# Seven edits to a four-layer transformer kernel: later FP4 weights, spreads of sixteen rows, carries copied by ScalarE, one masked product, stored positions

## The chip, the cores and the metric

The kernel runs on one core of a Trainium2 chip. The metric is the device time of one execution in microseconds (us), the median of three timed runs. The engines are named as in the profile: PE is TensorE (PEld its weight loads), DVE is VectorE, ACT is ScalarE, POOL is GpSimd, and SP is SyncE, which here only issues DMAs.

## The reference

Eight sequences of 1024 rows by 256 columns, all float32, pass through four blocks, each added to its input after a layernorm:

1. a decoder layer with causal linear attention of 16 heads of 16 columns, whose flows are normalised by running sums, followed by a GELU MLP 256 to 1024 to 256;
2. a ReLU MLP 256 to 1024 to 256;
3. softmax attention with one head of 256 columns over the 1024 rows;
4. a gated MLP 256 to 704 to 256, whose inputs and weights are rounded block by block to FP4 and back.

The part that the change touches most is the linear attention of block 1:

```python
sink_in  = normal / einsum(q + EPS, cumsum(k) + EPS)
src_out  = normal / einsum(k + EPS, cumsum(q) + EPS)
cons_sink = einsum(q + EPS, cumsum(k * src_out) + EPS) / normal
cons_src  = einsum(k + EPS, cumsum(q * sink_in) + EPS) / normal
src_comp = exp(clip(cons_src)) / cumsum(exp(clip(cons_src))) * normal
kv = cumsum(k (x) (v * src_comp));  x = (q * sink_in / normal) kv * sigmoid(cons_sink)
```

`normal` is the position in the sequence, 1 to 1024. The einsums sum over the 16 columns of a head.

## The kernel before

**Tiling.** A chunk is 128 rows, a group is G = 4 chunks (GT = 512 rows), and a sequence is NG = 2 groups, so there are 16 groups, p = 0 to 15. Group p runs through `linear_group(p)` (linear attention), `dense` (both MLPs of blocks 1 and 2, 64 steps of 256 rows by 128 hidden columns per group, each with its own pair of weight loads `w_ff`, five buffers deep), `norms_1` and `norms_2`. Then `soft_chunk` does blocks 3 and 4 chunk by chunk once a sequence has passed its two groups.

**Order of the work.** All of it is written out at build time by a planner, `Plan`. Parts are generators that yield what they need next (an engine, tiles, a free buffer, a due time `at`). `Plan.run` picks the part that waits least by a model of the engines, then the ripest, then by `at`, issues its instructions, and `Plan.took` (L157) books their modelled cost. Every engine's queue is then pinned to that order. So a step that is removed, added or priced differently can change the order of everything behind it, on every engine, SP's DMA queue included.

**Linear attention of a group.** `linear_span` (L919) projects q and k for all rows of its span, transposed: head and column on the partitions, row on the free axis. Tiles `cur[0..1]` are q, `cur[2..3]` are k. Then, in order:

- For each of the four tiles, a running sum (`running`, L806: one scan on DVE, and a copy of its last column into a carry for the next span if there is one) and a product with the tile of the other kind. `head_sums` adds 16 partitions of each head on PE.
- `flow` is position over these sums (L983). It has one row per head, and is needed on all 16 partitions of a head. In the first group, which is split in two spans (`near`), PE spreads it with masks. In the other 15 groups `spread` (L763) writes it to DRAM (`packed`) and reads it back four times with a repeating pattern (tiles `spread`, 128 x 512).
- Scale k and q by it, again four running sums and products, and `head_sums`.
- Clip, exp, a running sum on DVE, a reciprocal, and `scale` (L1040 to L1046), which is spread in the same manner to two tiles that scale q.

A carry is copied only where another span of the sequence follows: in both spans of group 0 and in every other even group, 8 times a span, 72 in all.

`linear_chunk` (L1079) then does the masked scores, the output, and the running k times v: the 32-column product `kvbank` is multiplied by a block-diagonal mask `bdiag` into `kv`, in two instructions (L1219), 112 in all.

**FP4 weights.** `fp4_weights` (L645) loads 18 pieces of the FP4 weights (`w_raw`), rounds them on DVE and ACT, and transposes them on PE. Piece i has `at = 0.9 + 2.2 i / 18`. In units of `at`, group p's linear work lies at p + 0.1 to p + 0.75, its dense work at p + 1 to p + 2, and the softmax of the first sequence from 3.

**Positions.** `pos` holds 1 to 512 as float; `rpos` is the reciprocal of position for both groups of a sequence (L501), made in `late_constants`.

Of the kernel before, what the change touches and what calls it, by code (L numbers as in the profile page):

```python
# [62 lines left out]
class Plan:  # L63
# [12 lines left out]
    def __init__(self, tc, nc):  # L76
# [15 lines left out]
        self.tiled = False  # L92
        self.parts = []
# [63 lines left out]
    def took(self, queue, op, args, kw):  # L157
# [44 lines left out]
        for ap in aps:  # L202
            name = ap.tensor.name
            if self.by.get(name) != queue:
                start = max(start, self.done.get(name, 0.0))
            if name not in self.done and name in self.held:
                start = max(start, self.used[name])
        end = start + cost
        if queue == "sync":
            n = 4e-6 / 160e-3  # L210
# [116 lines left out]
def block_stack_kernel(ctx: ExitStack, tc: tile.TileContext, a: dict, out: bass.AP):  # L327
# [115 lines left out]
    pos = const.tile([P, P], F32, name="pos")  # L443
    nc.vector.tensor_copy(pos, pos_i)
# [38 lines left out]
    def late_constants():  # L483
# [15 lines left out]
        for g in range(NG):  # L499
            yield dve()  # L500
            nc.vector.tensor_scalar(rpos[:, g, :], pos, float(g * GT), None, ALU.add)  # L501
            yield dve()
            nc.vector.reciprocal(rpos[:, g, :], rpos[:, g, :])
# [141 lines left out]
    def fp4_weights():  # L645
# [15 lines left out]
        for i, (src, turns) in enumerate(pieces):  # L661
            for j in range(i, min(i + 3, len(pieces))):
                if j not in raws:
# [3 lines left out]
                        dma(at=0.9 + 2.2 * i / len(pieces), when=lambda: count["stage"] == 4),  # L667
# [7 lines left out]
            at = 0.9 + 2.2 * i / len(pieces)  # L675
# [87 lines left out]
    def spread(packed, tiles):  # L763


        width = packed.shape[0] // 32 * P
        flat = hbm.tile([32, GT], F32, tag="packed", name="packed", bufs=4)
        yield dma(packed)
        nc.sync.dma_start(
            out=flat[:, :width].rearrange("r (t l) -> t r l", l=P), in_=packed  # L770
        )
        out = {}
        for b in tiles:
            t = out[b] = yield from fresh("flow", dma(flat), "spread")
            nc.sync.dma_start(
                out=t[:, :width],
                in_=bass.AP(
                    tensor=flat.tensor,
                    offset=flat.offset + 8 * b * GT,
                    ap=[[GT, 8], [0, DH], [1, width]],  # L780
# [25 lines left out]
    def running(out, cur, carry, b, first, last):  # L806
# [9 lines left out]
        if not last:  # L816
            nc.vector.tensor_copy(carry[:, b : b + 1], out[:, cur.shape[1] - 1 :])
# [101 lines left out]
    def linear_span(p, span, fronts, tiles):  # L919
# [48 lines left out]
        for n, b in enumerate((2, 0, 3, 1)):  # L968
            other = (b + 2) % 4
            prods[other] = yield from fresh(  # L970
                "flow", dve(cur[b], at=p + 0.15 + 0.04 * n + after, when=turn("flow")), "prod"
            )
            prod = prods[other][:, :width]
            running(prod, cur[b], past["cur"], b, opens, closes)
            yield dve(cur[other])
            nc.vector.scalar_tensor_tensor(prod, cur[other], ATT_EPS, prod, ALU.add, ALU.mult)
# [6 lines left out]
        nc.vector.scalar_tensor_tensor(flow, pos[rows], float(g * GT), r1, ALU.add, ALU.mult)  # L983
# [638 lines left out]
```

## Time and profile before

| what | value |
| --- | --- |
| time, median of three runs | 2690.91 us (2689.86 to 2692.45) |
| the profiled execution | 2683.94 us, of which the span from first to last instruction is 2682.2 us |
| mean granted PE clock | 0.991 |
| busy: PE, PEld, DVE | 2597.4, 2014.0, 1969.3 us |
| busy: ACT, POOL | 1246.7, 560.5 us |
| DMA | 209.92 MB, mean 78 GB/s |
| dense steps of group 0, first to last matmul of the first layer | 72.3 to 175.6 us |
| the same of groups 1, 2, 3 | 184.1 to 277.5; 286.2 to 432.1; 434.0 to 589.1 us |
| last dense step of group 15 | 2505.8 us |
| first softmax chunk starts; last one ends | 300.0; 2678.7 us |

Busy time is a sum over the whole span. The first group has the core to itself, the dense work starts at 72.3 us, the softmax chunks join at 300 us, and after 2505.8 us only softmax chunks are left. The time of the profiled execution is 1.74 us above its span and 6.97 us under the median of the runs.

In the rows of the profile, "idle before" or a figure in square brackets is the time for which the engine sat idle just before the instruction, and behind "<-" stands what ended it. Since every instruction goes through one helper, all lines read L308, and the tiles' names tell them apart.

### The profile page before, as it was taken

Reading aid. Unit: us, or ns where it says so; the run is one execution under the profiler, and the core shown is the slowest. Engines: PE = TensorE matmul, PEld = TensorE weight load, DVE = VectorE, ACT = ScalarE, POOL = GpSimd, SP = SyncE. Lnnn points to the kernel's source line nnn. Section 1 sums busy time; section 2 is a strip of 40 time slices with the busy share of each in tenths; the row PEclk is TensorE's granted clock in tenths of the full one; section 3 lists DMA queues with packets and bytes.
Section 4 is the critical chain, followed back from the end, with each engine's and each line's share of the span. In section 5 each row is a group of like instructions: output and inputs, shape, how many; then the busy total and the mean of one; then the engine's idle time right before and its main releaser. Section 6 shows DMA issues by size and latency. Waiting matters only on the chain.

```text
span 2682.2 us, 45602 instructions
## 1 busy us (share of the span) xinstructions
PE 2597.4 (97%) x16687; PEld 2014.0 (75%) x16687; DVE 1969.3 (73%) x4514; ACT 1246.7 (46%) x2430; POOL 560.5 (21%) x1101
## 2 busy tenths in 40 slices
PE   6999999999999999999999999999999999999997
PEld 4777777777777777777777777777777777787765
DVE  8889687776858668686776858778586776856576
ACT  2443445535455453645536354363635536344343
POOL 1232232221212213122131212212121131212000
PEclk8999999999999999999999999999999999999999
DMA  3334222312223222232322223132231322322100
GB/s 87 107 105 143 89 82 64 108 59 89 73 69 106 66 86 73 69 96 71 91 73 76 80 75 106 52 92 75 70 108 54 98 63 71 89 66 81 41 12 12
DMA packets 282135, 209.92 MB, mean 78 GB/s; under 512 B 23864, under 2 KB 270392, under 8 KB 281912
## 3 DMA queue, kind: packets, MB, share of 16 engines
q1 hardware_dynamic: 281912, 207.00, 25.9%
q8 instruction: 133, 2.18, 0.3%
q14 instruction: 90, 0.74, 0.1%
HBM read 188.17 MB, written 18.74 MB: 77 GB/s over the span
## 4 chain that ended last, share of the span: by engine, by line
PE 80%; DVE 12%; DMA 2%; issue 1%; ACT 1%; POOL 1%; SPq 0%; DVEq 0%; ACTq 0%
PE bank L308 80%; DVE hid L308 2%; DVE prod L308 1%; DVE n L308 1%; DVE ln_st L308 1%; DMA spread<-packed 1%; DVE x_amax L308 1%; DVE u L308 1%; DMA w_ff<-in_L_attn_W_dram 1%; DVE res L308 1%; POOL ln_rstd L308 1%; DVE div L308 1%; DVE e L308 0%; DVE q L308 0%; DVE ln_mv L308 0%
## 5 line engine op out<-in xcount | busy, mean ns | idle before, releaser
L308 PE MATMUL bank<-half,w_ff 128*128 128x256 f32 x2048 | 533.6, 383 | 14.5 <-DMA w_ff<-in_L_ffn_w_dram 6.0
L308 PE MATMUL bank<-w_ff,hidden 128*128 128x256 f32 x2048 | 530.4, 383 | 7.7 <-issue 6.6
L308 PEld LDWEIGHTS bank<-half,w_ff 128*128 128x128 f32 x2048 | 379.4, 191 | 91.4 <-issue 26.6
L308 PEld LDWEIGHTS bank<-w_ff,hidden 128*128 128x128 f32 x2048 | 371.1, 191 | 96.0 <-issue 50.7
L308 ACT ACT_TABLE_LOAD x308 | 395.2, 1283 | 75.2 <-PE bank L308 71.1
L308 POOL TENSOR_SCALAR ln_ve<-ln_mv 128x1 f32<-128x1 f32 x384 | 96.0, 250 | 1320.7 <-DVE ln_mv L308 1299.4
L308 ACT ACTIVATE hidden<-bank,c_L_ffn_b 128x256 f32<-128x256 f32 x256 | 121.1, 473 | 338.0 <-PE bank L308 336.7
L308 PE MATMUL bank<-n2T,qT 128*128 128x512 f32 x512 | 241.4, 594 | 0.9 <-ACT qT L308 0.9
L308 POOL TENSOR_TENSOR ln_rstd<-ln_ve,neghalf 128x1 f32<-128x1 f32 x384 | 229.4, 597 | 32.0
L308 PE MATMUL bank<-vt,probT 128*128 128x256 f32 x1024 | 232.2, 380 | 0.0
L308 PEld LDWEIGHTS bank<-vt,probT 128*128 128x128 f32 x1024 | 193.2, 190 | 30.3 <-issue 3.3
L308 ACT ACTIVATE hidden<-bank,c_L_attn_b 128x256 f32<-128x256 f32 x256 | 121.4, 474 | 177.0 <-PE bank L308 175.4
L308 PE MATMUL bank<-wdT,hqT 128*128 128x256 f32 x768 | 178.0, 382 | 1.8 <-ACT hqT L308 1.8
L308 PE MATMUL bank<-wgT,xqT 128*128 128x352 f32 x512 | 173.4, 461 | 1.1 <-ACT xqT L308 0.9
L308 PE MATMUL bank<-wuT,xqT 128*128 128x352 f32 x512 | 172.4, 459 | 0.0
L308 DVE TENSOR_TENSOR sc<-bank,triu 128x512 f32<-128x512 f32 x256 | 159.4, 679 | 5.3 <-PE bank L308 3.8
L308 PEld LDWEIGHTS bank<-wdT,hqT 128*128 128x128 f32 x768 | 145.4, 191 | 22.8 <-ACT hqT L308 2.8
L308 DVE TENSOR_TENSOR hid<-hid,bank 128x352 f32<-128x352 f32 x118 | 60.9, 516 | 133.8 <-PE bank L308 92.0
L308 POOL TENSOR_TENSOR xr<-xr,b_L_attn_ln_b 128x256 f32<-128x256 f32 x64 | 49.3, 788 | 482.6 <-DMA xr<-in_L_attn_inputs_dram 482.6
L308 PEld LDWEIGHTS bank<-n2T,qT 128*128 128x128 f32 x512 | 93.6, 190 | 69.5 <-issue 62.7
L308 PEld LDWEIGHTS bank<-wuT,xqT 128*128 128x128 f32 x512 | 97.3, 190 | 54.2
L308 PEld LDWEIGHTS bank<-wgT,xqT 128*128 128x128 f32 x512 | 92.6, 190 | 37.0 <-issue 3.8
(214 smaller groups left out, 4384.4 us busy)
## 6 DMA issues: line engine op xcount, KB each, us to landing
w_ff<-in_L_attn_W_dram SPq DMA_DIRECT2D x512, 128.0 KB
w_ff<-in_L_ffn_w_dram SPq DMA_DIRECT2D x512, 128.0 KB
spread<-packed SPq DMA_DIRECT2D x90, 256.0 KB
x<-in_L_attn_inputs_dram SPq DMA_DIRECT2D x64, 128.0 KB
xr<-in_L_attn_inputs_dram SPq DMA_DIRECT2D x64, 128.0 KB
rows<-res SPq DMA_DIRECT2D x64, 128.0 KB
out_dram<-y SPq DMA_DIRECT2D x64, 128.0 KB
rows<-rows SPq DMA_DIRECT2D x56, 128.0 KB
```

Of the source, the lines that this page charges most:

```text
L308: ins = method(*args, **kw)
```

## The change

Seven edits:

1. `spread` writes `packed` twice, side by side, into a DRAM tile of [32, 2, 512], and the four (or two) reads take a pattern of 16 rows, each repeated 8 times, where they took 8 rows, each repeated 16 times. Source and destination bytes of a spread stay 256 KB.
2. `running` leaves the copy of the carry to ACT, as a planned step of its own. In `linear_span` the four tiles go in two pairs: two scans, then the two products.
3. `pos` holds the positions of both groups; `rpos` and `flow` read it without an addition.
4. The two instructions that multiply e by position and by the row mask `src` become one.
5. The two masked products of k times v become one instruction of 256 elements.
6. The pieces of the FP4 weights have `at = 1.5 + 1.6 i / 18`.
7. The planner's model: a DMA moves 250 bytes per ns instead of 160, and PE costs twice as much for 2.1 us after more than 2 us of modelled idleness.

```diff
@@ Plan.took
+        if queue == "tensor":
+            if start - self.ran > 2.0:
+                self.slow = start + 2.1
+            if start < self.slow:
+                cost *= 2
+            self.ran = start + cost
         end = start + cost
         if queue == "sync":
-            n = 4e-6 / 160e-3
+            n = 4e-6 / 250e-3
@@ constants, late_constants
-    pos = const.tile([P, P], F32, name="pos")
-    nc.vector.tensor_copy(pos, pos_i)
+    pos = const.tile([P, NG, P], F32, name="pos")
+    for g in range(NG):
+        nc.vector.tensor_scalar(pos[:, g, :], pos_i, float(g * GT), None, ALU.add)
...
-            nc.vector.tensor_scalar(rpos[:, g, :], pos, float(g * GT), None, ALU.add)
-            yield dve()
-            nc.vector.reciprocal(rpos[:, g, :], rpos[:, g, :])
+            nc.vector.reciprocal(rpos[:, g, :], pos[:, g, :])
@@ fp4_weights (twice)
-            at = 0.9 + 2.2 * i / len(pieces)
+            at = 1.5 + 1.6 * i / len(pieces)
@@ spread
-        width = packed.shape[0] // 32 * P
-        flat = hbm.tile([32, GT], F32, tag="packed", name="packed", bufs=4)
+        flat = hbm.tile([32, 2, GT], F32, tag="packed", name="packed", bufs=4)
         yield dma(packed)
-        nc.sync.dma_start(
-            out=flat[:, :width].rearrange("r (t l) -> t r l", l=P), in_=packed
-        )
+        for e in range(2):
+            nc.sync.dma_start(out=flat[:, e, :].rearrange("r (t l) -> t r l", l=P), in_=packed)
...
-                    offset=flat.offset + 8 * b * GT,
-                    ap=[[GT, 8], [0, DH], [1, width]],
+                    offset=flat.offset + 8 * b * 2 * GT,
+                    ap=[[GT, 16], [0, DH // 2], [1, GT]],
@@ running
         if not last:
-            nc.vector.tensor_copy(carry[:, b : b + 1], out[:, cur.shape[1] - 1 :])
+            yield act(out)
+            nc.scalar.copy(carry[:, b : b + 1], out[:, cur.shape[1] - 1 :])
@@ linear_span, running sums of the tiles (those of the weighted tiles likewise)
-        for n, b in enumerate((2, 0, 3, 1)):
-            other = (b + 2) % 4
-            prods[other] = yield from fresh(
-                "flow", dve(cur[b], at=p + 0.15 + 0.04 * n + after, when=turn("flow")), "prod"
-            )
-            prod = prods[other][:, :width]
-            running(prod, cur[b], past["cur"], b, opens, closes)
-            yield dve(cur[other])
-            nc.vector.scalar_tensor_tensor(prod, cur[other], ATT_EPS, prod, ALU.add, ALU.mult)
+        for n, pair in enumerate(((2, 0), (3, 1))):
+            for b in pair:
+                need = dve(cur[b], at=p + 0.15 + 0.08 * n + after, when=turn("flow"))
+                prod = prods[(b + 2) % 4] = (yield from fresh("flow", need, "prod"))[:, :width]
+                yield from running(prod, cur[b], past["cur"], b, opens, closes)
+            for b in pair:
+                yield dve(cur[b], prods[b])
+                nc.vector.scalar_tensor_tensor(
+                    prods[b], cur[b], ATT_EPS, prods[b], ALU.add, ALU.mult
+                )
...
-        nc.vector.scalar_tensor_tensor(flow, pos[rows], float(g * GT), r1, ALU.add, ALU.mult)
+        nc.vector.tensor_tensor(flow, pos[rows, g, :], r1, ALU.mult)
...
-        nc.vector.scalar_tensor_tensor(e, pos[rows], float(g * GT), e, ALU.add, ALU.mult)
-        nc.vector.tensor_scalar(e, e, src[rows], None, ALU.mult)
+        nc.vector.scalar_tensor_tensor(e, e, src[rows], pos[rows, g, :], ALU.mult, ALU.mult)
@@ linear_chunk
-            for k in range(2):
-                nc.vector.tensor_tensor(
-                    new[:, k, :].rearrange("p (r d) -> p r d", r=4),
-                    kvbank[:, k, :].unsqueeze(1).to_broadcast([P, 4, 32]),
-                    bdiag.rearrange("p (r d) -> p r d", r=4),
-                    ALU.mult,
-                )
+            nc.vector.tensor_tensor(
+                new.rearrange("p k (r d) -> p k r d", r=4),
+                kvbank.unsqueeze(2).to_broadcast([P, 2, 4, 32]),
+                bdiag.rearrange("p (r d) -> p r d", r=4).unsqueeze(1).to_broadcast([P, 2, 4, 32]),
+                ALU.mult,
+            )
```

## The prediction

> **What bounds the kernel now.** I read the page's busy row first, then stretches of 67 us, then PE's timeline where the stretches lose time, then the DMA share microsecond by microsecond, then SP's timeline and the groups of instructions.
>
> ```profile
> PE 2597.4 (97%) x16687; PEld 2014.0 (75%) x16687; DVE 1969.3 (73%) x4514; ACT 1246.7 (46%) x2430; POOL 560.5 (21%) x1101
> ```
>
> PE is busy for all but 85 us. DVE's 73% costs time only where PE waits. So the question is where those 85 us lie (columns: stretch, length, busy us of PE, PEld, DVE, ACT, POOL, granted clock, DMA share, GB/s).
>
> ```profile
> 0.00:67.00 67.00, 41.45 (x318) 29.77 (x319) 56.23 (x151) 18.00 (x43) 13.07 (x35) 0.82 0.34 87
> 67.00:134.00 67.00, 62.27 (x441) 48.72 (x440) 53.95 (x129) 30.57 (x72) 18.64 (x37) 0.93 0.38 107
> 134.00:201.00 67.00, 64.02 (x575) 51.18 (x576) 58.90 (x146) 29.00 (x70) 26.09 (x47) 0.97 0.36 105
> 201.00:268.00 67.00, 60.37 (x381) 49.43 (x379) 60.52 (x148) 24.57 (x61) 16.32 (x32) 0.95 0.48 142
> 268.00:335.00 67.00, 63.38 (x537) 48.51 (x523) 45.16 (x103) 29.42 (x63) 17.11 (x32) 1.00 0.30 90
> 335.00:402.00 67.00, 66.87 (x476) 52.79 (x478) 55.48 (x127) 28.68 (x63) 20.41 (x38) 1.00 0.27 82
> ```
>
> The start loses 25.6 us while DVE is busy 84%: DVE bounds it. The next four stretches lose 4.7, 3.0, 6.6 and 3.6 us, and run below full clock. From 335 to 2450 us PE's gaps of over 0.4 us sum to about 18 us, none over 1.4; the last 200 us lose some 17 in the softmax chunks, which this change does not edit. So what the change can win lies before 335 us.
>
> PE's two longest waits after the start, from its timeline (start, duration, idle before in brackets):
>
> ```profile
> 135.00 2.07 PE L308 MATMUL bank<-half,w_ff 128*128 128x256 f32 x4 [5.72 <-DMA w_ff<-in_L_ffn_w_dram]
> 230.16 2.08 PE L308 MATMUL bank<-half,w_ff 128*128 128x256 f32 x4 [4.28 <-DMA w_ff<-in_L_attn_W_dram]
> ```
>
> Both wait for dense weights, and each comes just after the four spreads of group 1 and group 2. SP's timeline of the first, and the DMA share around a later spread of four that nothing crowds:
>
> ```profile
> 124.48 2.52 SPq L308 DMA_DIRECT2D spread<-packed  x4
> 128.08 6.32 SPq L308 DMA_DIRECT2D w_ff<-in_L_ffn_w_dram  x6
> ```
>
> ```profile
> 824.00:825.00 1.00, 1.00 (x5) 0.65 (x4) 0.00 (x0) 0.99 (x3) 0.09 (x1) 1.00 0.52 201
> 825.00:826.00 1.00, 1.00 (x6) 0.66 (x5) 0.33 (x1) 0.98 (x3) 0.00 (x0) 1.00 0.53 207
> 826.00:827.00 1.00, 1.00 (x7) 0.87 (x6) 0.97 (x2) 0.99 (x2) 0.00 (x0) 1.00 0.52 199
> 827.00:828.00 1.00, 1.00 (x6) 0.90 (x5) 0.93 (x3) 0.53 (x3) 0.00 (x0) 1.00 0.83 289
> ```
>
> Spreads alone hold the DMA share at 0.52: eight of sixteen engines work, at about 203 GB/s together. When weights join, the share rises and 289 GB/s flow. The landing records say the same: each spread ends in eight separate increments. The four of group 1 land 3.9 to 7.6 us after their own issues, and the weight load issued at 128.08 reaches eight engines by 132.8 and the other eight only at 134.96, when PE starts.
>
> **Part by part, against the profiled execution of 2683.94 us.**
>
> *Start (group 0).* These rows price what leaves DVE and what joins ACT:
>
> ```profile
> L308 DVE COPY carry_cur<-prod 128x1 f32<-128x1 f32 x36 | 5.5, 154 | 1.2
> L308 DVE SCALAR_TENSOR_TENSOR e<-pos,e 128x128 f32<-128x128 f32 (+1 forms) x17 | 5.3, 312 | 0.0
> L308 DVE TENSOR_SCALAR e<-e,src 128x128 f32<-128x128 f32 (+1 forms) x17 | 5.9, 346 | 0.6
> L308 DVE SCALAR_TENSOR_TENSOR e<-r,sink,e 128x128 f32<-128x128 f32 (+1 forms) x17 | 6.0, 350 | 0.6
> L308 ACT COPY ahead<-bank 128x1 f32<-128x1 f32 (+1 forms) x17 | 2.7, 158 | 8.0 <-PE bank L308 8.0
> ```
>
> A carry copy occupies DVE for 0.154 us and some 0.035 us of gap, 0.19; sixteen lie in the start: 3.0 us. The merged e step saves 0.31 us a span at full size (312 + 346 - 350 ns), about 0.2 on the half-size tiles, so 0.4 for two spans. Stored positions drop two additions of 0.21 us and add one conversion of 0.22: 0.2. Together 3.6 us of DVE work, at DVE's 84% share 3 us of time: **-3**. Bounds: +2 if the new order puts the second span's sums ahead of the first span's exp; -6 if PE, which ran at clock 0.50 from 30 to 50 us, is warmer too.
>
> *Spreads.* Four move 1.05 MB: 5.2 us at 203 GB/s, 3.6 us at the 289 that all engines reach. What is left waiting for weights shrinks by more than the difference, since the low eight engines also lag the high eight by 2.2 us, but `packed` now costs a second issue (0.57 us and a gap) before the spreads may go. The two waits sum to 10.0 us; after each PE ran 3.5 us at clock 0.50, about 1.8 us lost each time. All of it is 13.7 us. Evening out the engines alone gives back about 2 us of each wait, and a second wait near 2 us would keep its clock (PE's wait of 2.24 us at 334 us left the clock at 1.00). I take **-8**, bounds 0 and -13.7. For the other thirteen groups: PE waits of 0.51 us (508 us) and 1.11 us (1155 us) for weights behind spreads: **-1**, bounds 0 and -1.6. DVE's own 21.2 us of waiting for spreads in sixteen waits is nearly all off the path; the first spread lands little sooner, and the second issue takes that back.
>
> The Trainium skill ("DMA: Bandwidth & Descriptors", "Why a DMA increments its semaphore by 16 and not by 1") says that a DMA uses the largest number of engines up to 16 that divides the slowest dimensions of both its patterns. By that rule 8 rows against 128 partitions give the 8 of the trace and the new 16 rows give 16, while each `packed` write stays on 4, as its four increments in the trace have it; no run here shows the 16 yet.
>
> *FP4 weights.* Their 18 pieces take 40.7 us of DVE from 73 to 293 us, where DVE is 81 to 90% busy. Moved behind group 0's norms and group 1's linear work they free PE's four waits on DVE there (0.89, 0.74, 0.82 for `n`, 0.79 for `w_raw`: 3.2 us). But 18 pieces in 1.6 units instead of 2.2 are 1.4 times as dense beside group 2, where DVE works 60.5 of 67 us. I take **-1.5**, bounds -3.2 and +3. Lateness is covered: the last piece ends at 293.5 us and the first matmul on those weights is at 342.8 us. Past that the dense steps of group 2 (286 to 432 us) would hide a wait.
>
> *Carries as ACT steps.* In groups 2, 4 to 14 the copies are 56; off DVE they save 10.6 us, which PE never waits for there, since it has dense and softmax work. ACT gains 72 times 0.158 us, 11.4 us on an engine 46% busy. But the planner releases the next scan only once the copy has been placed: 0.06 us after the scan by its model, up to 0.5 us more for ripeness and one dense step of 0.9 us of PE. Eight carries in group 2 so cost its chain 0.5 to 12 us, less 1.5 for the copies gone. What is queued behind is group 2's own second scan, then `flow`, its DMAs and its chunks. Group 2 has no slack: its last needed transpose is at 284.6 us and its dense work starts at 286.2. In group 4 these are 575.2 and 593.0, so later groups have 18 us of cover. Group 1 copies nothing. I take **+1**, as DVE has other work ready in the gaps; bounds -1 and +10.
>
> *The rest.* One masked product of 256 elements for two of 128 (282 ns each) saves at most 0.1 us per chunk on DVE, off the path. The model of 250 GB/s is near the 289 measured. A cold PE at double cost changes the plan only where PE idles, at the start. Zero.
>
> *Sum*: -3 - 8 - 1 - 1.5 + 1 = -12.5 us on 2683.94, or 2671.4. The median lies 6.97 us above the profiled execution; I carry that over: **2678**.
>
> The skill ("TensorE: Matmul & The Clock Gate", "Part 1: The HAM clock gate") has the clock halve after an idle window of about 3.4 us. The rows here bracket that only between 2.24 and 4.28 us; by the rule a first wait left at 3 us would be free of the 1.8 us too, and the sum would be near -14.
>
> **Rivals.**
>
> *All early waits go* (2664): the spreads land in time, -13.7, -3.2, -1.6, and the start gives -6; -24.5, of which new gaps in the plan return some. For it: the waits share one cause. Against: group 1's stall was 5.7 us, more than evening out explains; the buffers of `w_ff` also set when loads start.
>
> *Nothing but the start* (2688, no change): the DMA gain of 8 to 10 us is eaten at group 2 by its gated carries, up to 10. For it: that missing slack of 1.6 us. Against: DVE is 90% busy there, so gaps are filled, and filled work is not lost.
>
> *Slower* (2708): spreads do not land sooner, because the repeated reads of DRAM or the issue of descriptors and not the number of engines limits them, while the planner now believes 4.2 us for four of them instead of 6.6. The steps that read weights are then placed up to 2.4 us too early in 15 groups: 4.8 us at groups 1 and 2, and half of 2.4 in each of the other 13, 15.6; less 3 at the start: +17. It decides if the fourth spread still lands over 7 us after its issue where weights follow (today 6.4 quiet, 6.8 to 7.6 crowded). For it: a load issued at 127.1 took 4 us even on the idle engines. Against: the share of 0.52, and 289 GB/s when all work.
>
> **How the numbers follow.** A measurement of this kernel can tell about 0.2%, 5.4 us, from no change, so faster means below 2685.5 and slower above 2696.3. Chances: forecast 0.50, with its own range 2668 to 2688; all waits gone 0.17; nothing but the start 0.16; slower 0.17, in which I count a plan that by its new order alone loses more than 5.4 us. Of the forecast's range about 0.02 falls above 2685.5. Faster is 0.65, same 0.18, slower 0.17. The range reaches to 2660, below the all-gone case by 4, and to 2702, within the slower case: some 0.1 is left above and 0.05 below.
>
> **What would show it.** Right: the DMA share near 1.0 in the microseconds of the spreads, sixteen increments each, the last landing under 6 us; no PE wait over 3 us at weights between 110 and 240 us; clock 1.00 there; the first dense step near 69 us instead of 72.3; no carry copy on DVE. Wrong: waits for weights after spreads in later groups too, a gap of PE before group 2's dense work, or FP4 pieces still running past 343 us. If the periodic part from 335 to 2450 us changes by more than 5 us, the cause is the new order and none of the terms above.

## The result and the profile after

The change makes the kernel slower, by 0.3%: 2698.68 us (2693.75 to 2706.22, 20 runs) against 2690.86 us (2683.52 to 2696.22, 20 runs) of the kernel before. The ratio is 1.0031, with a 95% interval of 1.0024 to 1.0038. The forecast was 2678 and faster. All ratios below are to the kernel before on the same chip; where a difference is given in us, it is (ratio - 1) x 2690. A ratio need not be exactly that of the two medians.

The page's busy row, after (its span is 2694.0 us; all lines read L315 now):

```profile
PE 2602.3 (97%) x16687; PEld 2020.0 (75%) x16687; DVE 1946.5 (72%) x4368; ACT 1253.7 (47%) x2504; POOL 585.9 (22%) x1101
```

DVE has 146 instructions and 22.8 us of work less. The work went as planned; the time did not follow. The same stretches as in the prediction, after:

```profile
0.00:67.00 67.00, 41.67 (x321) 30.72 (x321) 50.59 (x128) 20.25 (x59) 12.47 (x34) 0.84 0.31 87
67.00:134.00 67.00, 62.07 (x432) 48.73 (x433) 49.45 (x101) 28.79 (x63) 21.41 (x40) 0.93 0.36 103
134.00:201.00 67.00, 64.56 (x586) 51.76 (x585) 58.00 (x152) 28.99 (x71) 23.87 (x45) 1.00 0.37 110
201.00:268.00 67.00, 58.21 (x321) 46.80 (x323) 55.56 (x133) 25.59 (x70) 16.96 (x31) 0.90 0.47 135
268.00:335.00 67.00, 67.00 (x583) 51.91 (x576) 52.88 (x127) 32.31 (x71) 20.99 (x42) 1.00 0.35 100
335.00:402.00 67.00, 65.61 (x477) 52.01 (x476) 50.76 (x115) 29.08 (x65) 15.82 (x28) 1.00 0.28 81
```

DVE's first stretch is 5.6 us lighter (56.23 before), and PE gains 0.2 us from it. The third and the fifth stretch gained, the fourth lost 2.2 us and more of its clock (0.95 to 0.90). PE's waits of over 3 us from 110 to 290 us:

```profile
126.94 1.58 PE L315 MATMUL bank<-half,w_ff 128*128 128x256 f32 x4 [3.76 <-DMA w_ff<-in_L_ffn_w_dram]
...
231.10 2.07 PE L315 MATMUL bank<-half,w_ff 128*128 128x256 f32 x4 [3.93 <-DMA w_ff<-in_L_ffn_w_dram]
...
252.57 0.48 PE L315 MATMUL bank<-ident,scale 128*128 128x128 f32 x1 [4.18 <-DVE scale L315]
```

The two waits for weights shrank from 5.72 and 4.28, and a third wait of 4.18 us is new: group 2's chunks wait for `scale`. The larger part of the loss is later. From 335 to 2450 us, one row each of before and after (columns as above):

```profile
335.00:2450.00 2115.00, 2093.05 (x13520) 1628.87 (x13519) 1546.08 (x3502) 1023.20 (x1941) 453.35 (x881) 1.00 0.26 79
```

```profile
335.00:2450.00 2115.00, 2082.06 (x13456) 1620.97 (x13455) 1524.44 (x3374) 1022.62 (x1985) 471.70 (x870) 1.00 0.27 79
```

PE sat idle 21.95 us before and 32.94 after: 11.0 us more. The two spans differ by 11.8, but that the numbers are so close is in part chance. PE idled 4.1 us less outside this stretch, and over the whole span it was busy 4.9 us longer; 3.4 of these are two stretches at clock 0.50, from 707.75 and from 1356.29 us, which before does not have. The profiled execution of before is also one of its fastest: the ratio makes the loss 8.3 us. The prediction had named this sign: more than 5 us there means "the new order and none of the terms above".

What DVE waits for, after (total us, times, longest):

```profile
...
DVE prod L315 <- ACT carry_cur L315: 31.4, 15, 5.7
...
DVE spread L315 <- DMA spread<-packed: 22.0, 10, 3.8
...
DVE q L315 <- DMA spread<-packed: 11.4, 13, 2.5
...
DVE prod L315 <- ACT carry_w L315: 3.8, 11, 1.2
```

Before, the waits for spreads were 19.5 us (`spread`) and 1.7 (`q`), and those for ACT's carries did not exist. So there were two suspects. **ACT**: a product writes over the scan's tile, so DVE may not start it before ACT, whose queue has a fixed order too, has read the tile's last column; that wait was not in the prediction. **ORDER**: the planner's new list is worse, whoever copies; within it the **booking of DMAs** at 250 GB/s, by which the planner expects spreads earlier than they land.

### The profile page after: what moved, and what is told of

The parts are those of the page before. It is cut to its first block, busy times and chain, and to the rows that moved or that the text cites. A ratio compares the mean times of both kernels' runs of the same rounds, so it can differ in the third digit from the quotient of the medians.

```text
span 2694.0 us, 45517 instructions
## 1 busy us (share of the span) xinstructions
PE 2602.3 (97%) x16687; PEld 2020.0 (75%) x16687; DVE 1946.5 (72%) x4368; ACT 1253.7 (47%) x2504; POOL 585.9 (22%) x1101
## 4 chain that ended last, share of the span: by engine, by line
PE 75%; DVE 16%; DMA 3%; ACT 2%; issue 2%; POOL 1%; SPq 0%; DVEq 0%; ACTq 0%; POOLq 0%
PE bank L315 75%; DVE prod L315 3%; DVE hid L315 2%; DMA spread<-packed 2%; DVE ln_st L315 1%; DVE n L315 1%; DVE spread L315 1%; ACT L315 1%; DVE u L315 1%; DVE res L315 1%; DVE x_amax L315 1%; DVE mx L315 1%; DMA packed<-scale 1%; DVE ln_mv L315 1%; DVE div L315 0%
## 5 line engine op out<-in xcount | busy, mean ns | idle before, releaser
L315 PE MATMUL bank<-half,w_ff 128*128 128x256 f32 x2048 | 534.7, 384 | 16.8 <-DMA w_ff<-in_L_ffn_w_dram 7.7
L315 PE MATMUL bank<-w_ff,hidden 128*128 128x256 f32 x2048 | 534.7, 385 | 0.9 <-DVE u L315 0.6
L315 PEld LDWEIGHTS bank<-half,w_ff 128*128 128x128 f32 x2048 | 382.5, 192 | 91.3 <-issue 23.7
L315 PEld LDWEIGHTS bank<-w_ff,hidden 128*128 128x128 f32 x2048 | 370.1, 191 | 88.6 <-issue 41.1
L315 POOL TENSOR_SCALAR ln_ve<-ln_mv 128x1 f32<-128x1 f32 x384 | 101.0, 263 | 1500.5 <-DVE ln_mv L315 1486.3
L315 ACT ACTIVATE hidden<-bank,c_L_ffn_b 128x256 f32<-128x256 f32 x256 | 121.4, 474 | 297.0 <-PE bank L315 296.9
L315 POOL TENSOR_TENSOR ln_rstd<-ln_ve,neghalf 128x1 f32<-128x1 f32 x384 | 236.3, 615 | 32.0
L315 PE MATMUL bank<-n2T,qT 128*128 128x512 f32 x512 | 241.0, 594 | 0.9 <-ACT qT L315 0.9
L315 PE MATMUL bank<-vt,probT 128*128 128x256 f32 x1024 | 231.5, 379 | 0.0
L315 PEld LDWEIGHTS bank<-vt,probT 128*128 128x128 f32 x1024 | 192.6, 190 | 27.9 <-issue 1.9
L315 ACT ACTIVATE hidden<-bank,c_L_attn_b 128x256 f32<-128x256 f32 x256 | 121.4, 475 | 184.4 <-PE bank L315 182.5
L315 PE MATMUL bank<-wdT,hqT 128*128 128x256 f32 x768 | 178.1, 382 | 1.9 <-ACT hqT L315 1.9
L315 PE MATMUL bank<-wgT,xqT 128*128 128x352 f32 x512 | 174.3, 463 | 3.1 <-ACT xqT L315 2.9
L315 DVE TENSOR_TENSOR sc<-bank,triu 128x512 f32<-128x512 f32 x256 | 159.2, 681 | 20.5 <-PE bank L315 19.0
L315 PE MATMUL bank<-wuT,xqT 128*128 128x352 f32 x512 | 172.4, 459 | 0.0
L315 PEld LDWEIGHTS bank<-wdT,hqT 128*128 128x128 f32 x768 | 145.9, 192 | 22.8 <-ACT hqT L315 2.8
L315 PEld LDWEIGHTS bank<-n2T,qT 128*128 128x128 f32 x512 | 92.5, 190 | 68.5 <-issue 61.4
L315 DVE TENSOR_TENSOR hid<-hid,bank 128x352 f32<-128x352 f32 x116 | 59.7, 515 | 113.8 <-PE bank L315 72.0
L315 PEld LDWEIGHTS bank<-wuT,xqT 128*128 128x128 f32 x512 | 97.4, 190 | 54.0
L315 PEld LDWEIGHTS bank<-wgT,xqT 128*128 128x128 f32 x512 | 93.9, 190 | 45.5 <-issue 6.3
L315 DVE TENSOR_REDUCE mx<-bank 128x1 f32<-128x512 f32 x128 | 86.9, 679 | 46.7 <-PE bank L315 46.6
```

The costliest lines, as they stand in the source:

```text
L315: ins = method(*args, **kw)
```

## The experiments

All were timed beside the kernel before in five rounds. "Order kept" means that each queue has the very order of the kernel it starts from, the step in question apart; "planned again" means that the edit also gave a new order. The far pass is the time from the first issue of `packed` to the landing of the fourth `spread` (median of the 13 passes after 290 us, from issue and landing records). Its booked length follows from `Plan.took`: 0.4 us per issue, the bytes (65.5 KB each time `packed` is written, 262 KB each spread) at the booked rate, 1.8 us per landing. With one write at 160 GB/s that is 0.4 + 0.41 + 1.8 + 0.4 + 4 x 1.64 + 1.8 = 11.4; with two writes 11.8, at 250 GB/s 9.3.

| run | spread rows | far pass booked | measured | median us | ratio, interval |
| --- | --- | --- | --- | --- | --- |
| before | 8 | 11.4 | 11.5 | 2690.86 | 1 |
| the change | 16 | 9.3 | 10.7 | 2698.68 | 1.0031, 1.0024 to 1.0038 |
| a_dvecopy_locked | 16 | 9.3 | 10.5 | 2698.14 | 1.0035, 1.0021 to 1.0048 |
| b_actcopy_locked | 8 | 11.4 | 11.6 | 2699.57 | 1.0037, 1.0025 to 1.0049 |
| b_spread16_locked | 16 | 11.4 | 10.2 | 2688.54 | 0.9997, 0.9989 to 1.0006 |
| a_spread8_locked | 8 | 9.3 | 13.4 | 2715.75 | 1.0101, 1.0086 to 1.0116 |
| b_rate250 | 8 | 8.9 | 11.9 | 2706.89 | 1.0069, 1.0056 to 1.0082 |
| b_fp4later | 8 | 11.4 | 11.7 | 2690.01 | 0.9987, 0.9978 to 0.9996 |
| b_cold | 8 | 11.4 | 12.5 | 2696.27 | 1.0015, 1.0005 to 1.0026 |
| a_nocold | 16 | 9.3 | 10.3 | 2686.08 | 0.9990, 0.9981 to 0.9999 |
| a_noC | 16 | 9.3 | 10.4 | 2691.06 | 1.0009, 1.0000 to 1.0018 |
| a_oth160 | 16 | 9.3 | 10.3 | 2686.11 | 0.9993, 0.9982 to 1.0004 |
| a_latency | 16 | 10.7 | 10.1 | 2687.24 | 0.9990, 0.9981 to 0.9999 |
| a_rate160 | 16 | 11.8 | 10.3 | 2675.52 | 0.9956, 0.9943 to 0.9968 |
| a_sp160 | 16 | 11.8 | 10.2 | 2677.31 | 0.9956, 0.9943 to 0.9968 |
| a160_dvecopy_locked | 16 | 11.8 | 10.2 | 2676.32 | 0.9953, 0.9940 to 0.9965 |
| a160_spread8_locked | 8 | 11.8 | 12.4 | 2678.36 | 0.9961, 0.9947 to 0.9974 |
| a160_nocold | 16 | 11.8 | 10.1 | 2680.20 | 0.9964, 0.9952 to 0.9976 |
| a160_noF | 16 | 11.8 | 10.0 | 2683.66 | 0.9966, 0.9954 to 0.9979 |
| a160_noC | 16 | 11.8 | 10.4 | 2671.73 | 0.9933, 0.9921 to 0.9945 |

**1. Who copies the last column (order of the change kept).** The planner still books the copy on ScalarE.

```diff
-            nc.scalar.copy(carry[:, b : b + 1], out[:, cur.shape[1] - 1 :])
+            nc.vector.tensor_copy(carry[:, b : b + 1], out[:, cur.shape[1] - 1 :])
```

> The changed kernel with its order of instructions kept exactly, but each of the 72 copies of a last column is issued on VectorE in the place where ScalarE had it. Theory ACT (the product that overwrites the scan's tile waits for ScalarE's in-order queue to read the last column, 35.5 us of VectorE waits in the profile after, and ScalarE's own queue is held up behind it): VectorE takes back 35.5 us of waits for 72 x 0.18 = 13 us of work, so 5 to 13 us faster than the change, 2686 to 2694, and the waits 'prod <- carry' are gone. Theory ORDER (the list that the planner made is itself worse, whatever engine copies): within 4 us of the change, 2695 to 2703, with PE's waits of 1.0 to 1.6 us on VectorE in the odd groups still there.

Measured 1.0035: the same as the change. All 35.2 us of DVE's waits for ACT are gone and no time came back. Theory ACT falls for this order: the waits, less the 11 us of copies that DVE does instead, were worth nothing.

**2. The same step in the order of before (order kept).** The planner still books it on VectorE.

```diff
-            nc.vector.tensor_copy(carry[:, b : b + 1], out[:, cur.shape[1] - 1 :])
+            nc.scalar.copy(carry[:, b : b + 1], out[:, cur.shape[1] - 1 :])
```

> The kernel before with its order kept exactly, but each copy of a last column on ScalarE. Theory ACT: slower than before by 5 to 13 us, 2696 to 2704, with VectorE waiting some 30 us for the copies. Theory ORDER: within 4 us of before, 2687 to 2695. Before's order puts another tile's product between a scan and the overwriting of its tile less often than after's pairs do, so that by theory ACT the loss can be larger here than the change's.

Here ACT's copies cost 10 us (1.0037). The wait is real, and the order decides whether it counts. The products in this kernel (line, engine, operation, tiles, count | busy us, mean ns | us idle before, releasers):

```profile
L308 DVE SCALAR_TENSOR_TENSOR prod<-q,prod 128x512 f32<-128x512 f32 x60 | 41.7, 696 | 29.8 <-ACT carry_cur L308 24.7 <-ACT carry_w L308 3.6
L308 DVE SCALAR_TENSOR_TENSOR prod<-k,prod 128x512 f32<-128x512 f32 x60 | 41.1, 686 | 14.0 <-ACT carry_w L308 10.5 <-ACT carry_cur L308 2.9
```

and in the change, where two scans come first and then the product with k and the product with q. The product with k writes over the tile of the scan just before it, and has nearly all the waits; between the scan for the product with q and that product stand another scan of 1.3 us and the product with k:

```profile
L315 DVE SCALAR_TENSOR_TENSOR prod<-k,prod 128x512 f32<-128x512 f32 x60 | 41.2, 686 | 32.1 <-ACT carry_cur L315 29.5 <-ACT carry_w L315 2.3
...
L315 ACT COPY carry_w<-prod 128x1 f32<-128x1 f32 x36 | 6.9, 191 | 41.9 <-DVE prod L315 41.9
L315 ACT COPY carry_cur<-prod 128x1 f32<-128x1 f32 x36 | 5.7, 188 | 8.0 <-DVE prod L315 8.0
```

In the order of before, products of both kinds wait, 47.6 us in 65 waits against 35.2 us in 26. Its first dense step comes at 76.5 us, 4.2 us later than before, but by 335 us PE has idled no longer (43.3 us, 43.5 before). From 335 to 2450 us it idles 28.9 us, 7.0 more than before.

**3. Sixteen rows in the order of before (order kept).** The second write of `packed` is not booked.

```diff
-        flat = hbm.tile([32, GT], F32, tag="packed", name="packed", bufs=4)
+        flat = hbm.tile([32, 2, GT], F32, tag="packed", name="packed", bufs=4)
...
+        for e in range(2):
+            nc.sync.dma_start(out=flat[:, e, :].rearrange("r (t l) -> t r l", l=P), in_=packed)
...
-                    ap=[[GT, 8], [0, DH], [1, width]],
+                    ap=[[GT, 16], [0, DH // 2], [1, GT]],
```

> The kernel before with its order kept exactly, but `packed` is written twice and the spreads read 16 rows. The prediction's term: 8 us faster than before (bounds 0 and 13.7), 2683, with PE's waits for weights at 135 and 230 us near 2 us or less. Theory NOTHING (the second write of packed takes back what the 16 engines give; 5.7 and 4.3 us became 3.8 and 3.9 us in the change): 1 to 3 us faster, 2688 to 2690, and VectorE waits as long for its first spread as before.

Measured 0.9997: -0.8 us, and the interval reaches from -3.0 to +1.6. The fourth spread lands 4.79 us after its own issue where it took 6.67, but the second write of `packed` moves their first issue from 2.60 to 3.40 us behind the first issue of `packed`. The whole pass wins 1.3 us. PE's two waits for weights shrink to 3.70 and 3.31 us.

**4. Eight rows in the order of the change (order kept).**

```diff
-        for e in range(2):
-            nc.sync.dma_start(out=flat[:, e, :].rearrange("r (t l) -> t r l", l=P), in_=packed)
+        nc.sync.dma_start(out=flat[:, 0, :].rearrange("r (t l) -> t r l", l=P), in_=packed)
+        plan.took("sync", "dma_start", (), {"out": flat[:, 1, :], "in_": packed})
...
-                    ap=[[GT, 16], [0, DH // 2], [1, GT]],
+                    ap=[[2 * GT, 8], [0, DH], [1, GT]],
```

> The changed kernel with its order kept exactly, but one write of `packed` and spreads that read 8 rows. If 16 rows are worth the prediction's 8 us in this order too: 2704 to 2708. If they are worth the 2 us that the two first waits became shorter: 2699 to 2702. If the second write costs more than 16 engines give: faster than the change, under 2697.

Measured 1.0101: 19 us above the change, more than any of the three cases gave. So an order can depend on a transfer by 19 us that is worth 0.8 us in another order. Here a far pass took 13.4 us where 9.3 were booked.

**5. The planner's rate.** One number in the planner, planned again; a_rate160 is the change with this edit, b_rate250 the kernel before with the opposite one:

```diff
-            n = 4e-6 / 250e-3
+            n = 4e-6 / 160e-3
```

> The changed kernel planned again with one number put back: the planner books a transfer at 160 GB/s and not at 250. Every instruction is the same, the order is new. Theory RATE (the planner now believes that spreads land sooner than they do, 33.4 us of VectorE waits for spreads in the profile after against 21.2 before, and the steps behind them come late to TensorE): 8 us or more of the change's loss comes back, 2684 to 2692, and VectorE waits under 24 us for spreads. Theory PAIRS (the loss comes from ordering the products in pairs with two scans ahead): 2695 to 2702. Theory SCATTER (any edit of the plan moves the time by some microseconds either way, and no one part is to blame): 2685 to 2705, without a relation to the waits for spreads.

> The kernel before planned again with one number changed: a transfer is booked at 250 GB/s and not at 160. Every instruction is the same as before, spreads of 8 rows too. Theory RATE: slower than before by 8 to 20 us, 2699 to 2711, as the spreads here land still later (5.4 to 7.6 us after their issue), and VectorE waits over 35 us for them. Theory PAIRS: 2688 to 2694. Theory SCATTER: 2680 to 2700.

Both moved as theory RATE had it, not by its numbers throughout: a_rate160 came out 8 us below RATE's range, and in b_rate250 DVE waits 32.6 us for spreads, not over 35. With 160 the change is faster than before, 0.9956; with 250 the kernel before is 18.6 us slower than with 160. From 335 to 2450 us, a_rate160 and then b_rate250:

```profile
335.00:2450.00 2115.00, 2098.53 (x13566) 1636.01 (x13565) 1537.71 (x3419) 1058.74 (x2019) 465.62 (x887) 1.00 0.28 81
```

```profile
335.00:2450.00 2115.00, 2082.30 (x13485) 1617.96 (x13484) 1538.49 (x3487) 989.81 (x1913) 470.42 (x873) 1.00 0.26 79
```

PE idles 16.5 us at 160 and 32.7 at 250, beside 32.9 in the change and 21.95 before. In b_rate250 PE itself waits for what is queued behind the late spreads:

```profile
PE bank L308 <- DMA w_ff<-in_L_ffn_w_dram: 19.5, 11, 5.3
...
PE bank L308 <- DMA w_ff<-in_L_attn_W_dram: 9.7, 4, 4.2
```

That is 29.2 us in 15 waits; before it was 11.9 in 5. In the change it comes by way of DVE. Its DMA share and DVE's busy time (third figure with a count) during the spreads of a far pass in group 4, issued from 667.32 us:

```profile
669.00:670.00 1.00, 1.00 (x6) 0.90 (x5) 0.00 (x0) 0.00 (x0) 0.00 (x0) 1.00 0.95 313
670.00:671.00 1.00, 1.00 (x6) 0.87 (x6) 0.17 (x1) 0.00 (x0) 0.00 (x0) 1.00 1.01 248
671.00:672.00 1.00, 1.00 (x7) 0.82 (x6) 0.96 (x2) 0.00 (x0) 0.00 (x0) 1.00 1.03 240
672.00:673.00 1.00, 1.00 (x7) 0.92 (x6) 1.00 (x2) 0.73 (x2) 0.00 (x0) 1.00 1.06 247
```

All sixteen engines work, at 240 GB/s and more: as a rate, 250 is right. DVE waits all the same, 2.95 us for the first spread here. The second pass of that group, two spreads for q, on DVE's timeline after:

```profile
699.24 0.69 DVE L315 TENSOR_TENSOR q<-q,spread 128x512 f32<-128x512 f32 x1 [1.39 <-DMA spread<-packed]
700.32 0.69 DVE L315 TENSOR_TENSOR q<-q,spread 128x512 f32<-128x512 f32 x1 [0.38 <-DMA spread<-packed]
```

and what stands on PE's timeline some microseconds later:

```profile
706.43 0.41 PE L315 MATMUL bank<-ident,n 128*128 128x128 f32 x2 [1.40 <-DVE n L315]
707.93 2.08 PE L315 MATMUL bank<-half,w_ff 128*128 128x256 f32 x4 [1.09 <-DVE v L315]
```

The residual, `n` and `v` stand behind those two q products in DVE's queue. The clock falls to 0.50 at 707.75 us for 3.41 us. Four and eight groups later the same happens, after waits of q for spreads of 1.51 and 0.36 us (at 1347.56 and 1348.61) and of 1.48 and 0.57 us (at 1996.91 and 1998.17):

```profile
1354.73 0.41 PE L315 MATMUL bank<-ident,n 128*128 128x128 f32 x2 [1.49 <-DVE n L315]
1356.23 2.06 PE L315 MATMUL bank<-half,w_ff 128*128 128x256 f32 x4 [1.09 <-DVE v L315]
...
2004.29 0.41 PE L315 MATMUL bank<-ident,n 128*128 128x128 f32 x2 [1.68 <-DVE n L315]
2005.79 1.13 PE L315 MATMUL bank<-half,w_ff 128*128 128x256 f32 x4 [1.09 <-DVE v L315]
```

These six waits of PE sum to 7.8 us; before, no PE wait from 335 to 2450 us was over 1.33. That they come from the q products is read from the order of DVE's queue and was not tested alone. In a_rate160 the two q products of group 4 wait for nothing:

```profile
699.17 1.28 DVE L315 TENSOR_TENSOR q<-q,spread 128x512 f32<-128x512 f32 x2
```

DVE's other wait, for the first of four spreads, is 22.0 us in a_rate160 too. There the list gives PE more to do meanwhile: none of its waits for `n` or `v` in this stretch is over 0.6 us.

**6. Which transfers.** a_sp160 books `packed` and `spread` alone at 160 GB/s; a_oth160 has the two numbers exchanged.

```diff
-            n = 4e-6 / 250e-3
+            n = 4e-6 / (160e-3 if outs[0].tensor.name.startswith(("spread", "packed")) else 250e-3)
```

> The changed kernel planned again; only `packed` and `spread` are booked at 160 GB/s, every other transfer stays at 250. Theory LANDING (in the profile after, the far pass takes 10.7 us from the first issue of `packed` to the landing of its fourth spread, in the median of 13 passes; the planner at 250 GB/s books 4.8 us of fixed parts + 1.11 MB / 250 GB/s = 9.3 us, 1.5 us too little, at 160 GB/s 11.8): as good as all at 160, 2672 to 2682. Theory WEIGHTS (what costs time is that loads of weights and rows are believed too fast): 2692 or more. Theory SCATTER: 2675 to 2700, not tied to either.

> The counterpart of booking only `packed` and `spread` at 160 GB/s (2677.3 us): here these two stay at 250 GB/s and every other transfer is booked at 160. Theory LANDING: no better than the change, 2694 to 2704, with over 28 us of VectorE waits for spreads. If any plan other than the change's own is better than it (theory SCATTER, the change having drawn a bad one): 2676 to 2690.

The spreads alone bring everything back (0.9956), so the rate of the weights is not needed for it. But the counterpart is a miss: with the spreads at 250 it measured 0.9993, 10 us better than the change. So the change's own list is an unlucky one among those that book spreads too short, unless the rate of the other transfers helps where the spreads' is wrong; the runs do not part the two, and I call it scatter. The trace of a_sp160 also limits what the waits explain: q waits 6.9 us for spreads there and PE idles 21.60 us from 335 to 2450 us, more than a_oth160's 20.15, and yet it is 10 us faster.

**7. The right length at 250 GB/s.**

```diff
-            after = self.free["rings"] - end + 1.8
+            after = self.free["rings"] - end + 2.5
```

> The changed kernel planned again with 250 GB/s left, but with the fixed part of every landing booked at 2.5 us and not 1.8. The far pass is then booked at 9.3 + 2 x 0.7 = 10.7 us, what the profile after measures. Theory LANDING: most of the loss is gone, 2674 to 2687, with VectorE's waits for spreads under 27 us. Theory RATE ITSELF (160 is right for some other reason, such as queues of many weights): 2692 or more. Theory SCATTER: 2675 to 2700.

0.9990, 11 us better than the change, at the upper edge of what LANDING gave. But a_nocold and a_oth160, which book 9.3, lie as low, and the lists that book 11.8 lie lower. So this run does not show that a booking of the right length undoes the loss. It books 10.7 where 10.1 is measured; the lists at 11.8 book 1.4 to 1.8 us too much and are the fastest. That a longer booking helps for another reason than its being right stays a possibility.

**8. Parts taken out one at a time, at 250 GB/s.** a_noC has products one at a time and DVE's copies, as before; a_nocold leaves out the rule for a cold PE.

```diff
@@ a_noC, linear_span and running
-        for n, pair in enumerate(((2, 0), (3, 1))):
+        for n, b in enumerate((2, 0, 3, 1)):
...
-            yield act(out)
-            nc.scalar.copy(carry[:, b : b + 1], out[:, cur.shape[1] - 1 :])
+            nc.vector.tensor_copy(carry[:, b : b + 1], out[:, cur.shape[1] - 1 :])
@@ a_nocold, Plan.took
-        if queue == "tensor":
-            if start - self.ran > 2.0:
-                self.slow = start + 2.1
-            if start < self.slow:
-                cost *= 2
-            self.ran = start + cost
```

> The changed kernel planned again with the products as before: one scan and its product at a time, the last column copied by VectorE, no pairs. Theory PAIRS: the loss comes back, 2684 to 2692. Theory RATE: still slower than before by 5 us or more, 2695 to 2705, with VectorE waiting over 30 us for spreads. Theory SCATTER: 2685 to 2705.

> The changed kernel planned again without the rule that doubles TensorE's cost after an idle stretch. Every instruction is the same. The prediction had this at nothing outside the start: 2696 to 2701 in the theories RATE and PAIRS; in theory SCATTER 2685 to 2705. If the rule is itself the cause, since it pushes steps behind TensorE's gaps: 2692 or less.

Both are better than the change, 1.0009 and 0.9990, and both worse than the lists that book 160. Theory RATE had said 2695 or more for either; so it is not the whole of the loss. a_noC met theory PAIRS, and a_nocold the case that the rule itself is the cause. Leaving the rule out gave 11 us here, but the next two sets of runs do not bear that out: at 160 GB/s taking it out costs 2 us, and in the kernel before adding it costs 4.

**9. Parts taken out one at a time, at 160 GB/s.** First two with the order of a_rate160 kept (edits as in 1 and 4), then three planned again: a160_noC and a160_nocold with the edits of 8, and a160_noF.

```diff
@@ a160_noF, fp4_weights (twice)
-            at = 1.5 + 1.6 * i / len(pieces)
+            at = 0.9 + 2.2 * i / len(pieces)
```

> The changed kernel booked at 160 GB/s (2675.5 us) with its order kept exactly, the 72 copies of a last column on VectorE in the place where ScalarE had them. The profile there shows 15.0 us of VectorE waits for the copies, the changed kernel's 35.2. If ScalarE's copies cost nothing in the pairs' order: 2674 to 2677. If they cost what they did in the order of before (+10 us): 2666 to 2671. If VectorE misses the 72 x 0.19 = 14 us that it now works more: 2680 or more.

> The changed kernel booked at 160 GB/s (2675.5 us) with its order kept exactly, one write of `packed` and spreads of 8 rows. The planner books 11.8 us for a far pass here; with 8 rows it took 11.5 us in before and 13.4 in the changed order. Theory LANDING: at 11.5 to 13.4 measured against 11.8 booked the loss is small, 2676 to 2684, far from the 17 us that 8 rows cost at 250 GB/s. If 16 rows are worth 8 us or more in themselves: 2684 to 2693.

> The changed kernel booked at 160 GB/s and planned again, with the products one at a time and the last column copied by VectorE, as before. If the pairs with ScalarE's copies are what makes the change at 160 GB/s 13 us faster than before: 2684 to 2691. If they are worth nothing: 2673 to 2679.

> The changed kernel booked at 160 GB/s and planned again, without the rule that doubles TensorE's cost after an idle stretch. At 250 GB/s taking the rule out gave back 12.6 us. If the rule costs as much whatever the rate: 2662 to 2668. If it cost only beside spreads believed too fast: 2672 to 2680.

> The changed kernel booked at 160 GB/s and planned again, with the FP4 pieces due from 0.9 over 2.2 units, as before, and not from 1.5 over 1.6. The prediction had the later pieces at -1.5 us (bounds -3.2 and +3): then 2676 to 2679. If they are what makes the change faster at 160 GB/s: 2682 to 2690. If they are a loss beside group 2: under 2673.

ACT's copies again cost nothing in the pairs' order (0.9953 beside 0.9956), and 16 rows are worth 1.3 us (0.9961): booked long enough, they hardly matter. Without pairs and ACT's copies the kernel is faster still, 0.9933: the pairs cost here, which neither expectation allowed, and this is the fastest version, 2671.73 us. Taking them out gained 6 us at both rates (1.0031 to 1.0009, 0.9956 to 0.9933). The other two lose 2 to 3 us by their ratios, within what plans scatter (a160_noF's median alone, 2683.66, would fall in the case that the later FP4 pieces make the gain; experiment 10 gives them 3.5 us).

**10. Two edits alone in the kernel before**, each planned again: b_fp4later has the FP4 due times of the change, b_cold its rule for a cold PE.

```diff
@@ b_fp4later, fp4_weights (twice)
-            at = 0.9 + 2.2 * i / len(pieces)
+            at = 1.5 + 1.6 * i / len(pieces)
@@ b_cold, Plan.took
+        if queue == "tensor":
+            if start - self.ran > 2.0:
+                self.slow = start + 2.1
+            if start < self.slow:
+                cost *= 2
+            self.ran = start + cost
```

> The kernel before with one edit, planned again: the FP4 pieces are due from 1.5 over 1.6 units and not from 0.9 over 2.2. If the later pieces by themselves are worth what putting them back cost at 160 GB/s (8.1 us): 2680 to 2685. If they are worth the prediction's 1.5 us: 2687 to 2691. Plans that differ only in such an edit have scattered by some 6 us either way here, so a value of 2695 or more would show that those 8 us belong to one plan and not to the edit.

> The kernel before with one edit, planned again: the planner doubles TensorE's cost after an idle stretch. If the rule by itself is worth what taking it out cost at 160 GB/s (4.7 us): 2684 to 2688. If it costs time, as it did at 250 GB/s (12.6 us): 2696 to 2704. The prediction had it at zero: 2688 to 2692.

The later FP4 pieces gave 0.9987 (0.9978 to 0.9996), 2690.01 us, and the rule for a cold PE 1.0015 (1.0005 to 1.0026), 2696.27 us. Neither explains the gain at 160 GB/s.

**The runs together.** Four lists with 16 rows that book the spreads at 250 GB/s (the change, a_nocold, a_noC, a_oth160) lie at 0.9990 to 1.0031, mean 1.0006. The five that book them at 160 (a_rate160, a_sp160, a160_noC, a160_nocold, a160_noF) lie at 0.9933 to 0.9966, mean 0.9955. The groups do not touch; between their means are 0.51%, 13.7 us (11.4 without the change's own list), and within each a list moves the time by up to 11 us. The 18.6 us of b_rate250, the same edit in the kernel before, are more than that scatter.

## Why the prediction was wrong

**The step that failed is "The rest": "The model of 250 GB/s is near the 289 measured ... Zero."** It compared a rate with a rate, and as a rate it was right. The planner does not place steps by rates but by landings, and 160 GB/s, together with its fixed 0.4 and 1.8 us, had given the landing: 11.4 us booked, 11.5 measured. The change shortened the booking by 2.1 us (11.4 to 9.3) and the pass by 0.8 (11.5 to 10.7). Of the 1.5 us that are missing, 0.8 lie before the spreads: with two writes of `packed` they go 3.65 us after its first issue (booked 2.9). The other 0.7 lie from there to the fourth landing, 7.1 us (booked 6.4); the issues come 0.63 us apart (booked 0.4). This term measured +11 to +14 us as the difference of two groups of lists, not zero; the change's own list lies another 6 to 11 us above the three others that book alike, of which 6 may be the pairs of products and the rest has no cause in any run but scatter. That the shortened booking acts by readers placed too early is what the traces suggest; the one list booked near the measured length, a_latency, does not prove it. The working also took 335 to 2450 us, where PE idled 22 us, as a place where nothing could be won, and did not ask what could be lost there.

**The slower rival had the mechanism but a wrong condition.** It said that the planner at 250 GB/s places readers too early, and let this count only "if the fourth spread still lands over 7 us after its issue". The fourth landed 4.84 us after its issue, 5.8 at group 1, and the spreads still came later than the planner booked them, since `packed`'s hop and the spacing of issues belong to the length too. The rival's chance of 0.17 was too low for an edit that changes the order of everything.

**Spreads, -8**: the chain of reasons held and the size did not. Each spread now ends in sixteen increments, the DMA share is at 1, the last landing at group 1 is at 5.8 us instead of 7.6. This is the number of engines that the Trainium skill's rule gave ("DMA: Bandwidth & Descriptors", "Why a DMA increments its semaphore by 16 and not by 1"). But in a kept order it is worth 0.8 us (b_spread16_locked) or 1.3 (a160_spread8_locked), and 19 us in the change's own order (a_spread8_locked). The prediction wrote the second issue down and then did not take its 0.8 us off the pass; and the waits for weights have other causes, since in b_spread16_locked the first is still 3.70 us and loses the clock.

**Start, -3**: -0.5 us to the first dense step (72.3 to 71.8). With DVE's copies in the same order it starts at 70.0, so ACT's copies took 1.8 us of the gain.

**Carries, +1**: right for the copies in the change's order (0 in both orders of pairs), +10 in the order of before, the upper bound. The pairs themselves, for which the sum has no term, cost 6 us in both comparisons. The mechanism that was named, the planner's gate, is not the one the trace shows; it is the write after the read, 35.2 us of DVE waits, which nothing in the working had.

**FP4, -1.5**: -3.5 us alone (interval -5.9 to -1.1), inside its bounds but for 0.3 us. The last piece ends at 305.5 us, before 343.

**The sum.** -12.5 us was the forecast without a rate; with the spreads booked as before the change measures -11.8 us (-15.3 to -8.6). That is no proof of the terms: the spreads gave 1, not 8. Of where the gain comes from instead, the trace shows one place, 335 to 2450 us, where PE idles 16.5 us instead of 21.95, and the single edits do not show a cause: 16 rows -0.8, FP4 -3.5, the cold rule +4.0, pairs and ACT's copies a loss of 6. What is left (one masked product, stored positions, DVE's 22.8 us less work) was not tried alone. This stays open.

**Slips in the working.** The case that all early waits go is put at 2664; its own terms, -24.5 us on 2690.9, give 2666. Of the four stretches said to run below full clock, the last has 1.00. And the profile of before held a shorter wait that lost the clock than the 4.28 us of the bracket: 2.41 us, ended at 2667.05 us and followed by 3.41 us at 0.50. So to count on a wait near 2 us to keep its clock was a gamble.

**What should have shown it.** Right: the DMA share, sixteen increments, landings under 6 us, no carry copies on DVE. Wrong: waits over 3 us from 110 to 240 us were still there, the clock was 0.90 from 201 to 268 us, the first dense step was not at 69. The line on the periodic part named the place and the new order, though not what had made the order worse.

## What to carry to other kernels

A planner's cost for a transfer is tuned as a whole: before one number of it is made "truer", compare what it books from issue to landing, hops and issues included, with the landing records, because here booking 1 to 1.5 us too little cost more than booking 1.5 us too much. Then time it, since the list that booked nearest to the measured length was not the fastest. A transfer's worth depends on the order around it (16 rows: 0.8 us in one list, 19 in another), so measure an edit with the order kept, and an order against several of its neighbours. A wait of 30 us on an engine that is not the bound can be worth nothing; take it away in a kept order before blaming it.

## What the hardware showed that was not expected

PE's clock after a wait does not follow from the length of the wait alone. Over the 20 traces, all 34 waits of 3.46 us and more after the start came with a stretch at 0.50, which began in the wait or up to 1.1 us behind it and lasted 6.83 us in 24 cases and 3.41 in ten. Shorter ones went both ways. In a_oth160 a wait of 3.32 us kept its clock (the granted clock stands before the DMA share):

```profile
236.20:237.20 1.00, 1.00 (x5) 0.90 (x6) 0.82 (x1) 0.14 (x1) 0.00 (x0) 1.00 1.09 329
237.20:238.20 1.00, 1.00 (x7) 0.87 (x6) 0.92 (x2) 0.52 (x2) 0.55 (x1) 1.00 1.13 321
```

and in b_cold one of 2.00 us, after 8 us in which PE had not waited once for 0.4 us, lost it:

```profile
545.00:546.00 1.00, 0.00 (x0) 0.00 (x0) 0.97 (x3) 0.00 (x0) 0.00 (x0) 1.00 0.49 186
546.00:547.00 1.00, 0.14 (x1) 0.14 (x2) 0.93 (x4) 0.00 (x0) 0.33 (x2) 1.00 0.51 179
547.00:548.00 1.00, 1.00 (x4) 0.80 (x5) 0.97 (x3) 0.00 (x0) 0.84 (x2) 0.65 0.92 302
548.00:549.00 1.00, 1.00 (x4) 0.82 (x3) 0.26 (x2) 0.34 (x1) 0.66 (x2) 0.50 0.31 80
```

The Trainium skill ("TensorE: Matmul & The Clock Gate", "Part 1: The HAM clock gate") has the clock fall after an idle window of about 3.4 us that runs freely. The stretches of 3.41 and twice 3.41 us agree; a loss after 2.00 us of idleness does not fit a whole idle window, and here the measurement decides.

Reading the same DRAM rows eight times over does not hold the rate under 240 GB/s: in the rows of the far pass above, where spreads make up most of the traffic, 240 to 313 GB/s moved, against about 203 with 8 rows read 16 times.
